# Gathering the adjacency rows that hold something, instead of multiplying all 26 blocks

## The chip, the cores and the metric

The kernel runs on one core of one Trainium2 chip. The metric is the device time of one execution in microseconds (us), lower is better. A profile is one execution with the hardware profiler on; its span is up to 12 us off the median of the timed runs, so sums over stages use spans and verdicts use timed runs.

Engines in the profile: PE is TensorE (PEld its weight loads), DVE is VectorE, ACT is ScalarE, POOL is GpSimd, SP is SyncE. A "q" behind a name is that engine's sequencer, which also issues its DMAs.

## The reference, cut to what matters

`x` is 3327 nodes by 256 features, `adj` is 3327 by 3327 and sparse, all float32. The kernel pads 3327 to 26 blocks of 128.

```python
h = relu(layernorm(x))
R = (adj + I) / rowsum
Xf = Xa = h
for n in range(2):                       # "step 1" and "step 2" below
    A  = top_p_attention(Xa)             # softmax over 3327 nodes, smallest set with 90% of the mass
    Xf = R @ Xf                          # needs adj @ Xf
    Xa = A @ Xa
    Z += Xf @ U1[n].T + Xa @ U2[n].T
x = x + layernorm(h + Z) * g + b
h = relu(layernorm(x))
x = x + relu((d * adj * d.T) @ h @ W.T + bias)     # "stage 3"; d = rowsum ** -0.5
```

So adj is multiplied three times, over the same sparse pattern: 3 x 26 row blocks, each against all 26 column blocks. A row block's 128 rows of adj (transposed: 128 partitions, one per column node of a block) are empty in most (partition, block) places: with these inputs a partition has 7.65 places with something, of 26, on average, and at most 15.

## The kernel before

Per row block, adj arrives in four chunks and is multiplied in full:

```python
def adj_matmul(i, rhs, width):
    acc = ps_r.tile([P, 512], F32, tag="psr", name="adj_acc")
    for b0, nb in ADJ_CHUNKS:                          # 7 + 7 + 7 + 5 blocks
        a = big.tile([P, ADJ_BLOCKS, P], F32, tag="adj", name="adj_sb", bufs=3)
        nc.sync.dma_start(a[...], adj_t[i * P : (i + 1) * P, ...])
        for b in range(nb):
            nc.tensor.matmul(acc[:, :width], a[:, b, :], rhs[b0 + b][:, :width], ...)
    return acc

def tail1(i, e, den, xt):                              # after the attention of block i in step 1
    attend(e, den, h, xa1[i])                          # transpose e, multiply: "attend" below
    key_block(kt2, i, xa1[i])
    acc = adj_matmul(i, h, D + 1)                      # the last column gives the row sums
    t1 = acc[:, D] + 1.0; r_inv[i] = 1 / t1            # the "degree operation", VectorE
    propagate(acc, i, h, xf1[i])
# ... step 2 the same with xf1; stage 3: adj_matmul(i, h, D), scale, project, add, store
```

The attention itself is a chain on VectorE and ScalarE. In `prepare(i+1)` ScalarE exponentiates the logits and makes a start value; VectorE negates it (`nt`, "the negated threshold"), and ScalarE runs two counting passes (`ja`) over 3327 columns. VectorE then narrows the threshold with full-width passes (`scalar_tensor_tensor`, `max8`, `match_replace`). Which instruction stands where on each in-order engine is settled when the program is built, by the recording layer's own estimate of when things are ready.

## Time and profile before

| | us |
|---|---|
| median of 4 runs | 2593.8 (2592.5 to 2595.8) |
| span of the profile | 2595.4 |
| up to the first of the second full-width passes of step 1 | 118.0 |
| step 1, per row block | 36.5 |
| turn, last block of step 1 to first of step 2 | 76.8 |
| step 2, per row block | 42.9 |
| the rest, with stage 3 | 417.1 |

The stage times are starts of the second full-width pass over the scores (one per block and step), so "start", 25 periods of step 1, the turn, 25 periods of step 2 and the rest sum to the span.

### The profile page before, as it was taken

To read this page: it belongs to the slowest core of one execution; us is meant where nothing else is said; L and a number is where in the kernel's file an instruction comes from. 1 tells how busy PE (TensorE), PEld (TensorE's weight loads), DVE (VectorE), ACT (ScalarE), POOL (GpSimd) and SP (SyncE) were. 2 spreads that over 40 slices of the span, in tenths; PEclk is the share of its full clock that TensorE was granted. 3 is DMA by queue.
4 is the path that set the end of the run, shared out by engine and by line. 5 is a ranking of instruction groups with operands and counts; after the bars stand their busy time and mean duration, and the time that the engine had idled before them with its cause. 6 is when DMAs were issued, how large, how long until landed. Compare 5 with 4: busy or idle time off the path is not lost.

```text
span 2595.4 us, 29857 instructions
## 1 busy us (share of the span) xinstructions
PE 2303.9 (89%) x10458; PEld 1782.2 (69%) x10458; DVE 1704.9 (66%) x5071; ACT 971.9 (37%) x2315; POOL 61.2 (2%) x110
## 2 busy tenths in 40 slices
PE   5899999999999999969898989898989885899998
PEld 3677667776777677747676767676767664677776
DVE  3487787778777777488878887888788878000000
ACT  2534544554454444424434443444344433000000
POOL 1000000000000000000000000000000000000000
PEclk8899999999999999989999999999999997999999
DMA  3211111111111111211111111111111100244453
GB/s 106 80 39 46 48 53 39 46 49 52 39 46 53 48 39 53 69 29 43 49 39 54 43 49 39 53 43 49 40 53 43 49 24 9 82 144 140 141 143 102
DMA packets 66386, 153.77 MB, mean 59 GB/s; under 512 B 8116, under 2 KB 26290, under 8 KB 66226
## 3 DMA queue, kind: packets, MB, share of 16 engines
q1 hardware_dynamic: 63600, 149.97, 20.3%
q10 hardware_dynamic: 2626, 1.80, 0.2%
q8 instruction: 84, 1.38, 0.2%
q14 instruction: 76, 0.62, 0.1%
HBM read 144.93 MB, written 6.81 MB: 58 GB/s over the span
## 4 chain that ended last, share of the span: by engine, by line
DVE 53%; PE 30%; ACT 12%; issue 2%; POOL 1%; DMA 1%; ACTq 0%; POOLq 0%; SPq 0%
PE adj_acc L181 17%; DVE cand L335 8%; ACT ja L273 8%; DVE w L301 7%; DVE w L332 7%; DVE w L360 7%; PE att_acc L444 6%; DVE e L362 6%; PE p_t L436 3%; DVE cand L344 3%; DVE val L342 3%; ACT at L439 2%; POOL bn_rr L151 1%; PE p_xt_k L158 1%; PE p_o L541 1%
## 5 line engine op out<-in xcount | busy, mean ns | idle before, releaser
L181 PE MATMUL adj_acc<-h,adj_sb 128*128 128x257 f32 (+1 forms) x2704 | 674.4, 393 | 20.0 <-DVE h L529 10.1
L181 PEld LDWEIGHTS adj_acc<-h,adj_sb 128*128 128x128 f32 x2704 | 500.4, 195 | 98.6 <-issue 18.4
L181 PE MATMUL adj_acc<-xf,adj_sb 128*128 128x256 f32 x1352 | 371.8, 408 | 55.2 <-DVE prop L456 55.2
L439 ACT COPY at<-p_t 128x512 f32<-128x512 f32 (+1 forms) x364 | 184.4, 539 | 488.8 <-PE p_t L436 486.9
L444 PE MATMUL att_acc<-xa,at 128*128 128x256 f32 (+1 forms) x1352 | 334.3, 400 | 5.7 <-ACT at L439 5.7
L436 PE MATMUL p_t<-ident,e 128*128 128x128 f32 x1352 | 205.3, 296 | 136.7 <-DVE e L362 136.7
L444 PE MATMUL att_acc<-h,at 128*128 128x256 f32 (+1 forms) x1352 | 324.4, 391 | 0.6
L181 PEld LDWEIGHTS adj_acc<-xf,adj_sb 128*128 128x128 f32 x1352 | 257.1, 204 | 97.0 <-DVE prop L456 60.2
L273 ACT ACTIVATE ja<-e,nt 128x3327 bf16<-128x3327 f32 x104 | 319.2, 3070 | 5.0 <-DVE nt L269 3.8
L301 DVE SCALAR_TENSOR_TENSOR w<-e,t 128x3327 f32<-128x3327 f32 x78 | 287.3, 3683 | 46.9 <-ACT t L296 46.9
L444 PEld LDWEIGHTS att_acc<-xa,at 128*128 128x128 f32 (+1 forms) x1352 | 264.0, 200 | 65.6 <-ACT at L439 28.4
L444 PEld LDWEIGHTS att_acc<-h,at 128*128 128x128 f32 (+1 forms) x1352 | 258.6, 196 | 58.3 <-ACT at L439 22.9
L436 PEld LDWEIGHTS p_t<-ident,e 128*128 128x128 f32 x1352 | 177.0, 154 | 169.1 <-DVE e L362 151.9
L230 PE MATMUL p_l<-kt,q 64*128 64x512 f32 (+2 forms) x832 | 248.6, 555 | 7.2 <-ACT e L251 1.4
L335 DVE MAX8 cand<-w 128x8 f32<-128x208 f32 x832 | 251.3, 360 | 0.8
L546 DVE SCALAR_TENSOR_TENSOR o<-p_o,x_in 128x256 f32<-128x256 f32 x26 | 11.0, 424 | 345.6 <-PE p_o L542 345.6
L251 ACT ACTIVATE e<-p_l 128x512 f32<-128x512 f32 (+2 forms) x416 | 209.3, 514 | 72.9 <-PE p_l L230 70.2
L230 PEld LDWEIGHTS p_l<-kt,q 64*128 64x128 f32 x832 | 111.6, 185 | 150.3 <-ACT e L251 107.4
L332 DVE SCALAR_TENSOR_TENSOR w<-e,t 128x3327 f32<-128x3327 f32 x52 | 191.6, 3684 | 17.0 <-ACT t L296 16.9
L362 DVE SCALAR_TENSOR_TENSOR e<-w,kept,e 128x3327 f32<-128x3327 f32 x52 | 191.5, 3682 | 0.5
L360 DVE MATCH_REPLACE8 w<-kept,e 128x3335 f32<-128x3335 f32 x52 | 188.1, 3617 | 0.0
L284 DVE TENSOR_SCALAR n<-sign 128x1 f32<-128x1 f32 x52 | 7.9, 151 | 257.2 <-ACT ja L273 257.2
(350 smaller groups left out, 1795.2 us busy)
## 6 DMA issues: line engine op xcount, KB each, us to landing
adj_sb<-in_adj_t SPq DMA_DIRECT2D x234, 448.0 KB, 3.4
adj_sb<-in_adj_t SPq DMA_DIRECT2D x78, 320.0 KB, 2.9
x_in<-in_x SPq DMA_DIRECT2D x50, 128.0 KB, 2.0
x_hbm<-x_in SPq DMA_DIRECT2D x26, 128.0 KB, 2.0
x_in<-x_hbm SPq DMA_DIRECT2D x26, 128.0 KB, 2.1
out<-o SPq DMA_DIRECT2D x25, 128.0 KB, 1.7
u<-in_u1t ACTq DMA_DIRECT2D x2, 256.0 KB, 3.9
u<-in_u2t ACTq DMA_DIRECT2D x2, 256.0 KB, 5.0
```

The lines of the kernel that those rows point to most:

```text
L181: nc.tensor.matmul(acc[:, :width], a[:, b, :], rhs[b0 + b][:, :width], start=(b0 + b == 0), stop=(b0 + b == NB - 1),)
L230: nc.tensor.matmul(pl[:, :w], q[s * DA : (s + 1) * DA, :], kt[s * DA : (s + 1) * DA, c0 : c0 + w], start=True, stop=True,)
L251: nc.scalar.activation(e[:, at : at + w], pl[:, :w], AF.Exp, accum_out=zp[:, n : n + 1])
L273: nc.scalar.activation(ja, e[:, :N], f, bias=nt, accum_out=acc)
L301: nc.vector.scalar_tensor_tensor(jd, ev, t, ev, op0=ALU.is_gt, op1=ALU.mult, accum_out=mass)
L332: nc.vector.scalar_tensor_tensor(w[:, :N], ev, t, ev, op0=ALU.is_le, op1=ALU.mult, accum_out=below)
L335: nc.vector.max(cand[:, 8 * n : 8 * n + 8], w[:, c0 : c0 + cw])
L360: nc.vector.match_replace(w, kept, e, BIG)
L362: nc.vector.scalar_tensor_tensor(ev, w[:, :N], kept[:, 0:1], ev, op0=ALU.is_gt, op1=ALU.mult, accum_out=den)
L436: nc.tensor.transpose(pt[:kb, (b - g0) * P : (b - g0 + 1) * P], a[:, b * P : b * P + kb], ident)
L439: nc.scalar.copy(at[:, :full], pt[:, :full])
L444: nc.tensor.matmul(acc[:, :D], at[:kb, (b - g0) * P : (b - g0 + 1) * P], v[b][:kb, :D], start=(b == 0), stop=(b == NB - 1),)
```

## The change

Its intent: most of the 26 matmuls of a product multiply zeros. So for each row block, list on chip which (partition, block) places hold something, gather just those rows of adj and the matching rows of the operand by indirect DMA, and multiply 10 slots instead of 26 blocks. The list is made once, in step 1; the gathered adj rows go to memory and are reloaded in step 2 and stage 3. Nine slots are a partition's own, the tenth slot is shared: places beyond nine are spread over free partitions of it through a running count (`p_before`) and a permutation by matmul (`p_shared`).

```diff
+    def list_nodes(i):                                  # VectorE: 4 reduces over the dense row
+        for b0, nb, a in adj_chunks(i):                 # adj_sb now has bufs=2
+            nc.vector.tensor_reduce(most[:, b0 : b0 + nb], a[:, :nb, :], AX.X, ALU.max, apply_absolute_value=True)
+        ...                                             # 2 x (max, match_replace) over 26 codes
+        nc.tensor.matmul(before[:, 0:1], tri, count)    # p_before
+    def share_slots(i, codes, there, count, before):
+        nc.vector.tensor_scalar(at, slot_no[:, :OVER], before[:, 0:1], None, op0=ALU.add)   # at_slot
+        nc.vector.tensor_tensor(sel, slot_no..., at..., op=ALU.is_equal)                    # 128 x 896
+        nc.gpsimd.tensor_scalar(rows[:, :, 0], codes, -1.0, terms[:, 0:1], ...)
+        nc.gpsimd.tensor_scalar(rows[:, :, 1], codes, -float(P), terms[:, 1:2], ...)
+        for k in range(OVER):                                                               # p_shared
+            nc.tensor.matmul(shared[:, :2], sel[:, k, :], rows[:, REG + k, :], ...)
+        nc.scalar.copy(rows[:, REG, :], shared[:, :2])
+    def gather_adj(i, rows):
+        nc.gpsimd.tensor_scalar(a_idx, rows...); nc.gpsimd.tensor_scalar(v_idx[:, i, :], rows...)
+        for k in range(SLOTS):                                                              # 10
+            nc.gpsimd.indirect_dma_start(ac[:, k, :], None, adj_t..., a_idx[:, k : k + 1])
+        nc.sync.dma_start(ac_hbm[i * P : (i + 1) * P], ac...)
+    def gather_nodes(i, hbm, width):                                                        # 10
+        for k in range(SLOTS):
+            nc.gpsimd.indirect_dma_start(vg[k][:, :width], None, hbm[:, :], v_idx[:, i, k : k + 1])
+    def adj_gathered(ac, vg, width):
+        for k in range(SLOTS):
+            nc.tensor.matmul(acc[:, :width], ac[:, k, :], vg[k][:, :width], ...)
...
+        def ahead1(i):                                  # in the middle of block i
+            gather1(i + 1); lists[i + 2] = list_nodes(i + 2)
         def tail1(i, e, den, xt):
             attend(e, den, h, xa1[i])
             key_block(kt2, i, xa1[i])
-            acc = adj_matmul(i, h, D + 1)
+            rows[i + 2] = share_slots(i + 2, *lists.pop(i + 2))
+            acc = adj_gathered(*parts.pop(i), D + 1)
...
+        # stage 3: odd blocks gathered, even blocks dense as before
```

Further parts: the reciprocal roots move from GpSimd (`pow`) to ScalarE (Ln, Exp), `h` and step 1's result xf go through memory, and the counting passes write uint8 in place of bf16. The lists hold 16 places a partition and 128 shared ones a block; the kernel checks this at its end, and repeats the whole network dense where it fails. With these inputs they fit (at most 15 places and 75 shared ones).

## The prediction

> **What bounds the kernel now.** I first cut the run into its stages and read the busy time of each engine in each (start:end in us, length, then busy us and instruction counts per engine, granted TensorE clock, DMA share, GB/s):
>
> ```profile
> core 0: us, PE busy (x) PEld busy (x) DVE busy (x) ACT busy (x) POOL busy (x), PEclk, DMA share, GB/s
> 118.00:1030.00 912.00, 849.31 (x3960) 650.57 (x3959) 697.01 (x2041) 428.57 (x997) 16.53 (x24) 0.97 0.17 48
> 1030.00:1107.00 77.00, 74.40 (x349) 57.39 (x348) 38.48 (x115) 31.47 (x77) 0.00 (x0) 1.00 0.25 72
> 1107.00:2215.00 1108.00, 949.46 (x4283) 733.77 (x4282) 910.20 (x2686) 441.99 (x1050) 27.44 (x50) 0.92 0.14 41
> 2215.00:2595.00 380.00, 345.77 (x1545) 281.08 (x1543) 15.48 (x40) 24.38 (x58) 1.09 (x2) 0.98 0.45 128
> ```
>
> The first row is attention step 0 ("step 1" below), then the turn to step 2, step 2 itself, and the last layer ("stage 3"), which multiplies by adj and little else. Each has 26 row blocks. The starts of the second full-width pass over the scores lie 36.2 to 37.2 us apart in step 1 (I use 36.6), some 40.4 and 45.7 us in turn in step 2 (mean 42.9), and stage 3 repeats every 14.0 us.
>
> TensorE is 93% busy in step 1, and that invites the belief that it is the bound. So next I asked what VectorE waits for, over the whole run (us in total, times, longest):
>
> ```profile
> DVE o L546 <- PE p_o L542: 345.6, 26, 14.0
> DVE n L284 <- ACT ja L273: 257.2, 38, 7.1
> ...
> DVE prop L456 <- PE adj_acc L181: 3.8, 2, 3.4
> DVE t L490 <- PE adj_acc L181: 1.8, 1, 1.8
> ```
>
> The first line is stage 3. In steps 1 and 2 the large wait is for ScalarE's two counting passes; the waits for the adj product come to 5.6 us in 52 blocks. So those products are filler: they run in TensorE's gaps and seldom hold VectorE. The order of VectorE's work in one block shows its chain (start, duration, instruction, idle before it and its releaser):
>
> ```profile
> 640.12 3.62 DVE L360 MATCH_REPLACE8 w<-kept,e 128x3335 f32<-128x3335 f32 x1
> 643.77 3.68 DVE L362 SCALAR_TENSOR_TENSOR e<-w,kept,e 128x3327 f32<-128x3327 f32 x1
> ...
> 656.77 0.15 DVE L284 TENSOR_SCALAR n<-sign 128x1 f32<-128x1 f32 x1 [6.48 <-ACT ja L273]
> ```
>
> It is full except for this 6.5 us hole. TensorE in stage 3 is the opposite case:
>
> ```profile
> 2404.04 10.63 PE L181 MATMUL adj_acc<-h,adj_sb 128*128 128x256 f32 x48
> 2415.32 0.44 PE L158 MATMUL p_xt_k<-ident,prop 128*128 128x128 f32 x2 [0.65 <-ACT prop L537]
> 2415.59 1.03 PE L181 MATMUL adj_acc<-h,adj_sb 128*128 128x256 f32 x4
> 2416.46 1.03 PE L541 MATMUL p_o<-w_l,xt_k 128*128 128x256 f32 x4
> 2417.42 0.69 PE L542 MATMUL p_o<-b_l,ones_row 1*128 1x256 f32 x2
> ```
>
> One float32 matmul is two passes, so a product is 52 of them: 11.1 us (52 x 0.2137, the mean from dividing a long run of such matmuls) plus 2.2 us of projection and some 0.7 us of gaps, which is the 14.0. Only here is the adj product the bound.
>
> **What the Trainium skill says.** "Perfetto Trace Analysis", section Identifying the Most-Contended Engine, says that matmul busy share does not tell how near TensorE is to its limit. The trace agrees: 93% busy in step 1, and yet hardly waited for. "DMA: Bandwidth & Descriptors", section SWDGE vs HWDGE vs iDMA, says that GpSimd's DMAs have their descriptors computed in software by a GpSimd core, with a single queue; its section Latency and other measured facts puts the first byte at about 1 us, against 0.6 us on the hardware path, and names the emission of descriptors as the reason. The trace of before cannot confirm either: it has no GpSimd DMA at all (its queues are "hardware_dynamic" and instruction fetches). Its SyncE loads of 448 KB land after 3.4 us, its 128 KB transfers after 1.7 to 2.1 us.
>
> **The change, part by part.**
>
> *Removed.* 16 of 26 matmuls per product: 16 x 2 x 0.2137 = 6.84 us of TensorE per product, in all 52 blocks of steps 1 and 2 and in the 13 odd blocks of stage 3. (26 + 26 + 13) x 6.84 = 445 us of TensorE time, but by the above only stage 3's share is on the path.
>
> *Stage 3.* Even blocks stay at 14.0 us, and may lose some 0.5 us because adj now has two buffers for three: a chunk of 7 takes 7 x 0.4275 = 3.0 us to use and 3.4 us to land. Odd blocks become 14.0 - 6.84 = 7.2. A pair takes 21.7 in place of 28. 13 pairs are 282; with a few us at either end 285 to 295 in place of 380: **-85 to -95**, if the 10 gathers of a pair fit in its 21.7 us.
>
> *VectorE in step 1.* New per block: four reduces over the dense adj row; from a 1664-element reduce of the run before at 1.874 us I take 896 x 1.13 ns = 1.0 us plus a little, so three at 1.08 and one of 640 at 0.82: 4.06. Lists (two rounds of max and replace over 26 codes, some ten small operations) about 1.6, the 128x896 comparison 1.08, a few smalls 0.4: about 7.1 us. In the order of the built program 5.4 of it (reduces and lists) stands between the negated threshold and the counts, that is, in the 6.5 us hole. VectorE's own chain stays near 37 to 38.
>
> *The gather loop of step 1.* This decides. Per block GpSimd makes two index operations and issues 20 indirect DMAs of 128 rows (10 of adj, 10 of the operand) in order. In the built program's order TensorE has, in this sequence: the gathered product A(i), then attend(i-1), the projection for the keys, then the small `p_shared` matmuls that finish the list for block i+1; ScalarE copies these into `rows`; GpSimd's indices for i+1 wait for that copy; A(i+1) waits for the last gather. Engines go in order, so this is a closed ring, once per block:
> - 20 gathers: 20T, with T the GpSimd time of one;
> - landing of the last: about 2.3 us (a 128 KB transfer lands in 1.7 to 2.1 above); its matmul 0.6;
> - attend: 20.6 (from 647.52, the first transposition, to 668.2, the end of its last matmul in before);
> - projection to the end of the keys: 2.7 (to about 670.6, with the adj filler between);
> - 7 small matmuls 1.2, copy 0.6, two GpSimd operations 1.2 (one of 128x1 took 0.55 in before).
>
> Sum: 20T + 29.2. VectorE does not escape: its degree operation behind A(i) also stands right after the last pass over the scores of block i-1, so it stops until A(i) is there. T is in no trace of mine. My estimate is 1.1 us, from the skill's 1 us of emission above, and from the diff gathering only every other block in stage 3: gathering all would make a block the larger of 7.2 and 10T, against 21.7 / 2 = 10.9 with half of them, so the author's choice makes sense only for a T of about 1.1 or more. With T = 1.1 the ring is 51.2, against 36.6: 25.5 periods x 14.6 = **+372**. T = 0.6 gives 41, 0.8 gives 45, 1.5 gives 59.
>
> *Step 2.* The gathers need only the list kept from step 1 and rows in memory, so they run a block ahead: 10T = 11 us of GpSimd in 42.9. VectorE's order is nearly as before: about 0. The reciprocal root moves from GpSimd (0.55 us a call) to two ScalarE operations: 0 to 10 over the run, taken as 0.
>
> *Ends.* The turn took 77 us against a period of 43 with TensorE full; less adj work there gives about -10. At the start of step 1 the first two lists and 20 gathers stand before block 0: about +20.
>
> Sum: 2594 + 372 - 90 - 10 + 20 = 2886; I say **2890 us**.
>
> **The rivals.**
> (a) *Cheap gathers*: with T at most 0.4 the ring is 37 us and hides under VectorE; only stage 3 moves: about 2500. For it: descriptor work may be pipelined within the queue. Against it: the skill's figure, and that stage 3 is half dense.
> (b) *GpSimd's throughput alone*: if my reading of the ring is wrong and the gathers run ahead freely, the period is max(37, 20T + 1.2). At T = 1.1 nothing changes in step 1 and the total is about 2510; at T = 2 it is 41 and the total near 2620. Against it: the built order itself.
> (c) *TensorE is the bound, as its busy share suggests*: then all 445 us come off: about 2150. The wait table speaks against it.
> (d) *The two adj buffers*: reduces wait for loads of 3.4 us per chunk, queued on SyncE behind stores that wait for gathers. The hole absorbs some; worth +2 to +5 per block, 50 to 130 in all, on top of (a) or (b), and mostly hidden inside the ring.
>
> **Range and chances.** T from 0.7 to 1.5 gives rings of 43 to 59, totals of about 2685 to 3095; with (d) a little more above: 2690 to 3130. Faster by over 2% (below 2541) needs T under about 0.5 or no ring: 6%. Within 2% needs T near 0.5 or a mix of (a) with (d): 7%. Slower: 87%.
>
> **What would show it.** The starts of the second full-width pass in step 1 about 51 us apart. VectorE's degree operation waiting for the gathered product, over 10 us a block, the largest new wait of the run; TensorE's gathered product waiting for gather DMAs; GpSimd issuing for 22 us of each period and idle for the rest, its index operations waiting for ScalarE's copy of `rows`. Stage 3 in pairs of about 22 us, step 2 unchanged near 43. It is wrong if GpSimd's 20 gathers take under 9 us or over 30, if they start before the attend of the block before has ended, or if the degree operation does not wait. If GpSimd never idles in step 1, (b) holds and the ring is not the reason.

## The result, and the profile after

| | before | after |
|---|---|---|
| median, us | 2593.8 | 3121.9 (4 runs, 3116.3 to 3135.3) |
| ratio | | 1.204 (95%: 1.200 to 1.208) |

A ratio is the mean time of one kernel's fast runs over that of the other's in the same rounds, so it is not quite the ratio of the medians quoted. The change is slower by a fifth. That lies inside the predicted range, near its upper end (3130).

The stages of the profile after, in the same columns as the table in the prediction (step 1, turn, step 2, rest):

```profile
198.00:1572.00 1374.00, 955.43 (x3528) 645.15 (x3528) 816.65 (x2384) 440.60 (x1068) 555.13 (x574) 0.74 0.25 73
1572.00:1681.00 109.00, 77.25 (x251) 49.98 (x249) 37.86 (x107) 32.44 (x77) 44.98 (x46) 0.70 0.24 73
1681.00:2717.00 1036.00, 807.74 (x3526) 599.93 (x3526) 884.16 (x2580) 454.90 (x1140) 345.82 (x214) 0.93 0.18 56
2717.00:3114.00 397.00, 301.17 (x1223) 229.68 (x1221) 38.59 (x105) 30.54 (x76) 123.24 (x130) 0.90 0.43 131
```

In step 1 no engine is full any more: TensorE 70%, VectorE 59%, ScalarE 32%, GpSimd 40%. When nothing is full and the time is longer, the engines wait for one another, perhaps in a circle. Who waits for whom, over the run and all engines (us in total, times, longest):

```profile
POOL a_idx L288 <- ACT rows L281: 757.6, 25, 88.2
...
DVE t L641 <- PE adj_acc L317: 320.4, 23, 17.9
DVE o L729 <- PE p_o L725: 244.2, 18, 20.7
PE adj_acc L317 <- DMA vg<-h_hbm,v_idx: 240.9, 121, 9.7
...
DVE n L417 <- ACT ja L406: 63.0, 11, 7.1
```

The old large wait (the counting passes, 257.2) has shrunk to 63.0, and the degree operation `t`, which waited 1.8 us in all before, now waits 320.4, some 14 us each time. It waits for the gathered product, that waits for gathers, and GpSimd's index operation waits for `rows`, once per block. One turn of the circle, from GpSimd's timeline and then TensorE's:

```profile
746.78 1.03 POOL L292 DMA_INDIRECT ac<-in_adj_t,a_idx  x1 [0.27 <-POOL v_idx L289]
748.12 0.95 POOL L292 DMA_INDIRECT ac<-in_adj_t,a_idx  x1 [0.30 <-issue]
...
773.94 0.95 POOL L308 DMA_INDIRECT vg<-h_hbm,v_idx  x1 [0.30 <-issue]
...
802.33 0.26 POOL L288 TENSOR_SCALAR a_idx<-rows 128x10 int32<-128x10 f32 x1 [26.82 <-ACT rows L281]
```

```profile
776.01 2.23 PE L317 MATMUL adj_acc<-vg,ac 128*128 128x257 f32 x4 [0.33 <-DMA vg<-h_hbm,v_idx]
778.03 1.50 PE L569 MATMUL p_t<-ident,e 128*128 128x128 f32 x8
...
799.15 0.71 PE L328 MATMUL p_k<-xt_k,w 128*128 128x128 f32 x4 [0.46 <-ACT xt_k L199]
800.30 1.70 PE L280 MATMUL p_shared<-rows,sel 128*128 128x2 f32 x14 [0.44 <-ACT kt L333]
```

Twenty gathers from 746.8 to 774.9, the last two slots' matmuls to 778.2, attend and the key projection to 799.9, the shared-slot matmuls to 802.0, and GpSimd, idle for 26.82 us, starts the next indices at 802.33: 56.4 us after the last time (745.93). The turn is a typical one: the mean over 21 turns of step 1 is 56.1 us, with 27.9 for the gathers.

Where the time went, by the five stage numbers of the two profiles:

| stage | before | after | difference |
|---|---|---|---|
| start | 118.0 | 198.0 | +80.0 |
| step 1, 25 periods | 911.7 (36.5 each) | 1374.3 (55.0 each) | +462.6 |
| turn | 76.8 | 108.9 | +32.1 |
| step 2, 25 periods | 1071.8 (42.9) | 1035.3 (41.4) | -36.5 |
| rest | 417.1 | 397.9 | -19.2 |
| span | 2595.4 | 3114.5 | +519.0 |

### The profile page after: what moved, and what is told of

It is laid out like the page before. It is cut to its first block, busy times and chain, and to the rows that moved or that the text cites. A ratio compares the mean times of both kernels' runs of the same rounds, so it can differ in the third digit from the quotient of the medians.

```text
span 3114.5 us, 28889 instructions
## 1 busy us (share of the span) xinstructions
PE 2231.8 (72%) x8794; PEld 1582.5 (51%) x8794; DVE 1857.8 (60%) x5442; ACT 1019.7 (33%) x2549; POOL 1113.0 (36%) x1026
## 4 chain that ended last, share of the span: by engine, by line
issue 31%; PE 28%; DVE 17%; POOL 10%; ACT 7%; DMA 5%; another core or an unknown queue 1%; SPq 0%; POOLq 0%; ACTq 0%
PE att_acc L577 11%; POOL ac L292 5%; PE adj_acc L225 4%; POOL vg L308 4%; PE adj_acc L317 4%; DVE w L493 3%; DVE e L495 2%; DMA vg<-h_hbm,v_idx 2%; ACT ja L406 2%; PE p_t L569 2%; DMA adj_sb<-in_adj_t 2%; DVE w L434 2%; PE p_l L363 1%; ACT at L572 1%; DVE cand L468 1%
## 5 line engine op out<-in xcount | busy, mean ns | idle before, releaser
L317 PE MATMUL adj_acc<-vg,ac 128*128 128x256 f32 (+1 forms) x1300 | 467.2, 498 | 303.5 <-DMA vg<-h_hbm,v_idx 240.9
L308 POOL DMA_INDIRECT vg<-xf_hbm,v_idx x260 | 393.7, 1514 | 635.3 <-PE adj_acc L317 559.1
L317 PEld LDWEIGHTS adj_acc<-vg,ac 128*128 128x128 f32 x1300 | 278.2, 237 | 464.4 <-issue 231.4
L577 PE MATMUL att_acc<-xa,at 128*128 128x256 f32 (+1 forms) x1352 | 355.6, 418 | 49.1 <-ACT at L572 48.0
L406 ACT ACTIVATE ja<-e,nt 128x3327 uint8<-128x3327 f32 x104 | 319.3, 3070 | 57.1 <-DVE nt L402 42.3
L363 PE MATMUL p_l<-kt,q 64*128 64x512 f32 (+2 forms) x832 | 303.7, 698 | 34.1 <-ACT q L357 22.8
L308 POOL DMA_INDIRECT vg<-h_hbm,v_idx x260 | 281.1, 1081 | 87.9 <-issue 71.6
L292 POOL DMA_INDIRECT ac<-in_adj_t,a_idx x260 | 284.0, 1092 | 78.3 <-issue 67.8
L434 DVE SCALAR_TENSOR_TENSOR w<-e,t 128x3327 f32<-128x3327 f32 x78 | 287.3, 3684 | 19.6 <-ACT t L429 16.0
L308 POOL DMA_INDIRECT vg<-hn_hbm,v_idx x130 | 123.2, 948 | 375.2 <-DMA hn_hbm<-h 186.3
L225 PE MATMUL adj_acc<-h,adj_sb 128*128 128x256 f32 x676 | 171.2, 410 | 54.4 <-DMA adj_sb<-in_adj_t 44.7
```

The costliest lines, as they stand in the source:

```text
L225: nc.tensor.matmul(acc[:, :width], a[:, b, :], rhs(b0 + b)[:, :width], start=(b0 + b == 0), stop=(b0 + b == NB - 1),)
L292: nc.gpsimd.indirect_dma_start(ac[:, k, :], None, adj_t.rearrange("r (b n) -> (r b) n", n=P), bass.IndirectOffsetOnAxis(ap=a_idx[:, k : k ...
L308: nc.gpsimd.indirect_dma_start(vg[k][:, :width], None, hbm[:, :], bass.IndirectOffsetOnAxis(ap=v_idx[:, i, k : k + 1], axis=0))
L317: nc.tensor.matmul(acc[:, :width], ac[:, k, :], vg[k][:, :width], start=(k == 0), stop=(k == SLOTS - 1))
L363: nc.tensor.matmul(pl[:, :w], q[s * DA : (s + 1) * DA, :], kt[s * DA : (s + 1) * DA, c0 : c0 + w], start=True, stop=True,)
L406: nc.scalar.activation(ja, e[:, :N], f, bias=nt, accum_out=acc)
```

## The experiments

All experiments were right in their results unless said otherwise. Their stage numbers, to be read with the texts below:

| kernel | median us | start | step 1 each | turn | step 2 each | rest |
|---|---|---|---|---|---|---|
| before | 2593.8 | 118.0 | 36.5 | 76.8 | 42.9 | 417.1 |
| after | 3121.9 | 198.0 | 55.0 | 108.9 | 41.4 | 397.9 |
| e1_order | 2968.3 | 195.8 | 49.1 | 102.1 | 41.4 | 402.0 |
| e2_half (wrong on purpose, one look) | 2861.1 | 170.2 | 45.7 | 107.0 | 41.5 | 402.3 |
| e3_bufs (one look) | 3058.2 | 196.2 | 55.4 | 96.8 | 41.5 | 342.4 |
| e4_dense1 | 2936.2 | 131.5 | 50.8 | 98.8 | 41.5 | 404.4 |
| e5_behind | 2703.1 | 155.2 | 42.9 | 86.4 | 41.5 | 355.6 |
| e6_ring1 (one look) | 3109.5 | 156.6 | 58.9 | 88.5 | 41.4 | 355.4 |
| v1 | 2576.7 | 124.9 | 38.9 | 111.7 | 42.0 | 316.4 |
| v2 | 2494.3 | 120.6 | 36.5 | 97.5 | 41.6 | 313.3 |
| e7_spare (one look) | 2598.4 | 118.2 | 36.6 | 93.0 | 42.2 | 413.7 |

### e1_order: the gathered product moved behind the attend

```diff
+    with tc.issue_after(last_shared[i + 1]):     # queue on TensorE behind p_shared of block i+1
         acc = adj_gathered(*parts.pop(i), D + 1)
```

> Only the place of the gathered product of block i on TensorE changes: in step 1 (blocks 1 to 24) it is queued behind the shared-slot matmuls of block i+1, so after the attend of block i-1. Ring theory: nothing in the list for block i+1 waits for block i's gathers any more, GpSimd's 28 us per block run beside everything else, and the period of step 1 falls from 55.0 us to 37 to 40; the run to about 2690 to 2780 us. Rival 1 (GpSimd's own throughput sets the period) and rival 2 (VectorE's new list work sets it): the period stays at 50 or more, the run within 2% of 3122.

Measured: 2968.3 us, ratio to before 1.144; step 1 at 49.1 us on average and 51 in its steady part. A miss for both sides: the ring was cut where the theory said, the run gained 154 us, and step 1 was still 13 us a block above the kernel before. Two waits of VectorE's timeline in this run show what took its place:

```profile
820.19 0.23 DVE L268 TENSOR_SCALAR at_slot<-slot_no,p_before 128x7 f32<-128x7 f32 x1 [7.24 <-PE adj_acc L320]
...
835.79 0.19 DVE L253 MAX8 codes<-most 128x8 f32<-128x26 f32 x1 [5.71 <-issue]
```

The first is a 0.23 us operation of the list for a later block. It stands in VectorE's queue just before the `match_replace` that ends the present block, and it waits for `p_before`, a matmul on one column, which stands on TensorE behind the logits. (The built program lets it wait for nothing else; `adj_acc` is only what the profile shows at its release.) Not all of its wait is queue order: in most blocks of this run it is released 2 to 10 us after the end that the profile models for `p_before` (820.2 against 817.7 here), with little or no work shown on TensorE in the longer of these stretches. Why TensorE was late there is left open. The second begins as GpSimd's two small list operations end (835.76), which stand in GpSimd's queue behind the 20 gathers (in the built order this instruction has a semaphore wait on GpSimd, so the "issue" of the profile, meaning that it saw no releaser, is this wait). So the trace suggests a second circle, through the bookkeeping of the list: attend, logits and `p_before` on TensorE, `at_slot` before the end of the block on VectorE, the next attend.

### e2_half: half the gathers in step 1

```diff
-        for k in range(SLOTS):            # in gather_adj, and likewise in gather_nodes for step 1
+        for k in range(0, SLOTS, 2):
```

> Wrong results on purpose: step 1 gathers 5 + 5 rows per block in place of 10 + 10 and multiplies 5; order and list work as in the changed kernel. Ring theory: each gather stands on the ring with its 1.25 us, so the period falls by 10 x 1.25 plus some 1.5 us of the occasional slow gather, from 55 to 41 to 42, and the run to about 2770 us. If the gathers were beside the path: no change. If VectorE's list work is the bound: no change.

Measured: 2861.1 us, step 1 at 45.7 us a block, alternating between 43 and 49. The gathers are on the path, as they should be, but ten of them gave back 9.3 us where the ring alone promised 13 to 14. The trace shows what kept the rest. Over 21 turns the gathers take 13.9 us on average in place of 27.9, but the attend begins 7.9 us after the last gather in place of 3.2, because now TensorE waits for `e`, the pass with which VectorE ends a block (waits from 400 to 1300 us):

```profile
PE p_t L573 <- DVE e L499: 89.9, 10, 13.1
```

In the changed kernel this wait does not occur between 400 and 1300 us. So a second path, through VectorE, holds the period about 5 us above what the ring alone would give here; e5 and e6 then take the two apart.

### e3_bufs: three buffers for adj

```diff
-    a = big.tile(..., tag="adj", name="adj_sb", bufs=2)     ... tag="vg", bufs=14
+    a = big.tile(..., tag="adj", name="adj_sb", bufs=3)     ... tag="vg", bufs=10
```

> Three buffers for adj as in the kernel before, ten for gathered operand rows in place of fourteen. If the two adj buffers cost stage 3 its gain: a pair of blocks takes 21.7 to 22.5 us in place of 25.5, and the run falls by 40 to 50 us; the ring of step 1 stays at 55. Rival: the loads stand in SyncE's queue behind the store of the previous output, whatever their number: pairs stay at 25 to 26, the run the same.

Measured: 3058.2 us; a pair of blocks of stage 3 takes 21.4 us in place of 25.5, and step 1 does not move (55.4). The run fell by 64 us, more than the 40 to 50 expected: the rest by 55.5, of which 11 are in the first pair of blocks, and the turn by 12. An even, dense block of stage 3 on TensorE, first in the changed kernel and then here:

```profile
2850.67 5.45 PE L225 MATMUL adj_acc<-h,adj_sb 128*128 128x256 f32 x24
2859.82 7.13 PE L225 MATMUL adj_acc<-h,adj_sb 128*128 128x256 f32 x24 [3.71 <-DMA adj_sb<-in_adj_t]
```

```profile
2853.97 10.92 PE L225 MATMUL adj_acc<-h,adj_sb 128*128 128x256 f32 x48
```

With two buffers TensorE stops for 3.71 us in the middle of the block, and the second half then takes 7.13 us for the 5.45 of the first: after a pause the same matmuls are slower. The Trainium skill, "TensorE: Matmul & The Clock Gate", Part 1, says that the clock follows how busy TensorE has been, and the traces agree: the granted clock over the slower half is 0.76, over the first half 1.00; and in e5_behind, where the pause is 1.29 us, the 24 passes after it take 5.45. So a stall can cost more than its length. In step 1 the granted clock fell from 0.97 before to 0.74 after; the prediction had left this out. With three buffers there is one run of 48. The prediction had allowed 0.5 us for this. A later run shows that the number of buffers is only a part of this: e5_behind has two buffers too, and stops for only 1.3 to 1.5 us (22.6 us a pair), because there the load of the third chunk was issued when the first chunk was through, at 2497.1 for a block begun at 2492.2; in the changed kernel it was issued only when the second was, at 2856.2 for a block begun at 2848.2. So the count of buffers costs about 1 us a pair, and which of the two the third chunk was given costs the other 3. That the recording layer gave it the wrong one is read from these issue times, not tested by itself.

### e4_dense1: step 1 multiplies all 26 blocks again

```diff
-    acc = adj_gathered(*parts.pop(i), D + 1)
+    acc, lists = list_nodes(i, lambda b: h[b], D + 1)   # dense product and reduces over the same chunks
+    gather_adj(i, share_slots(i, *lists))               # 10 gathers, for step 2 and stage 3 only
```

> Step 1 multiplies all 26 blocks again, and still makes the lists and gathers the adj rows (10 indirect DMAs a block) for step 2 and the last layer; steps 2 and 3 as in the changed kernel. 6.84 us more TensorE work per block and no product waits for a gather. Ring theory: step 1's period is VectorE's chain, 37 to 39; no 80 us at the start; the run about 2540 to 2620. Rival 2 (VectorE's list work sets the period): 7 us on top of 36.6, so 43 to 45, the run 2700 or more. TensorE as the bound: slower than the changed kernel, over 3122.

Measured: 2936.2 us, ratio 1.130; step 1 at 50.8. The start fell to 131.5, as expected, but with no product waiting for any gather, step 1 was as slow as in e1. VectorE and SyncE in one period:

```profile
774.65 1.09 DVE L253 TENSOR_REDUCE most<-adj_sb 128x7 f32<-128x896 f32 x1 [7.60 <-DMA adj_sb<-in_adj_t]
```

```profile
755.98 0.33 SPq L644 DMA_DIRECT2D xf_hbm<-xf  x1
769.68 0.33 SPq L302 DMA_DIRECT2D ac_hbm<-ac  x1
770.17 1.36 SPq L214 DMA_DIRECT2D adj_sb<-in_adj_t  x2
```

SyncE issues nothing for 13 us: the store of the gathered rows stands at the head of its queue and waits for the gathers to land, and the loads of adj stand behind it; 0.5 us after the store they go. VectorE's reduce waits 7.60 us for such a load, with the negated threshold behind it. So the gathers reached VectorE through a third in-order queue. That is the first half of step 1. From the block at 871 us on, the reduces hardly wait for chunks, and the next list waits in their place, 4.9 to 11.5 us a block:

```profile
1079.21 0.19 DVE L259 MAX8 codes<-most 128x8 f32<-128x26 f32 x1 [11.52 <-issue]
```

It begins as GpSimd's two list operations end (1079.18), which stand behind the block's gathers, as in e1_order, and the period stays at 49 to 54 us up to the last two blocks. So one queue held step 1 in the first half and the other in the second. My first theory, that the ring closes through the product alone, fell here.

### e5_behind and e6_ring1: the bookkeeping out of the way, with and without the product's ring

e5_behind is e1_order with the list's work placed where VectorE idles, the two list operations taken from GpSimd, and the store on GpSimd's queue. e6_ring1 is the same with only e1's edit undone.

```diff
+    with tc.issue_after(last_nt[0]):                 # VectorE: behind the negated threshold
         lists[i + 2] = list_nodes(i + 2)
+    with tc.issue_after(last_e[0]):                  # VectorE: behind the pass that ends the block
         at_slot, crowd, sel
-    nc.gpsimd.tensor_scalar(rows[...]) x2
+    nc.vector.tensor_scalar(rows[...]) x2
-    nc.sync.dma_start(ac_hbm[...], ac)
+    nc.gpsimd.dma_start(ac_hbm[...], ac)
```

> e1_order left step 1 at 51 us. Theory now: a second ring, through VectorE's and GpSimd's queues. VectorE's slot operation stands before the pass that ends block i (match-replace and e) and waits for the small count matmul, which stands on TensorE behind the logits; and GpSimd's two list operations stand behind 20 gathers, with VectorE's next list waiting for them. This kernel is e1_order with the list work placed where VectorE has its hole (behind the negated threshold), the two list operations on VectorE, and the store of the gathered rows on GpSimd's queue. If the second ring is all: step 1 at 38 to 41 us, the run at 2700 to 2770. Rival: GpSimd's descriptor writing and VectorE's passes hold each other up, whatever the order: 47 or more, the run over 2880.

> e5_behind, with only the gathered product put back to its old place (before the attend of the block before). The ring of the prediction alone: 28 us of gathers, 3 of landing and last matmul, 20 to 22 of attend, 4 to 6 of projection, shared-slot matmuls and indices: 54 to 57 us a block, the run 3080 to 3160, as slow as the changed kernel although nothing of the second ring is left. If the prediction's ring were not binding by itself: under 50, the run under 3000.

Measured: e5_behind 2703.1 us, ratio 1.042; step 1 at 42.9 (the run inside what was expected, the period 2 us over it). e6_ring1 3109.5 us, step 1 at 58.9, 2 us over the 54 to 57 expected: the attend takes 22.4 us on average there, 19.0 in the changed kernel. With the changed kernel and e1 this makes a square for the period of step 1:

| | product before the attend | product behind it |
|---|---|---|
| list work as built | 55.0 (after) | 49.1 (e1) |
| list work moved | 58.9 (e6) | 42.9 (e5) |

Either circle alone holds the period at 49 or more (in e1_order some of it may be TensorE's unexplained lateness); only without both does it fall. That is why cutting the one that the prediction named gave so little by itself, and it also refutes the rival that GpSimd's descriptor writing and VectorE's passes hold each other up to 47 us or more whatever the order. The second row changes three things at once (places on VectorE, GpSimd's list operations, the queue of the store), so what each of them is worth is not shown. What keeps e5 6 us above the kernel before is in its waits: over the run VectorE waits 90.8 us for adj chunks and 76.2 for exponentials.

### v1 and v2: a version that beats both

If gathers in step 1 only cost, step 1 can stay dense, and the list be made there with no hurry: it is wanted only in step 2. v1 does this (lists one to two blocks behind, behind the negated threshold), with e5's store, three adj buffers, and two of every three blocks of stage 3 gathered. v2 adds two repairs that v1's profile asked for.

```diff
 v1, step 1 (from e4_dense1):
+    if i > 1: gather_adj(i - 2, share_slots(i - 2, *lists.pop(i - 2)))
+    if i:     lists[i - 1] = code_nodes(i - 1, mosts.pop(i - 1))     # all behind last_nt on VectorE
+    acc, mosts[i] = list_nodes(i, lambda b: h[b], D + 1)
 v1, stage 3:
-    if sparse and i % 2:
+    if sparse and i % 3:                  # gathered rows in the idle score tiles
 v2:
-    adj_sb bufs=3, vg bufs=10
+    adj_sb bufs=5, vg in the same buffers, three rows to a tile
-    lists and gathers of blocks 24 and 25 in the turn
+    in blocks 1 and 2 of step 2
```

> Made to beat both: step 1 dense as in e4_dense1, lists one to two blocks behind and in VectorE's hole, store of gathered rows on GpSimd's queue, three adj buffers, and in the last layer two of every three blocks gathered (20 gathers = 25 to 27 us of GpSimd in 14.0 + 7.2 + 7.2 = 28.4 us). Ring theory: step 1 at 37.5 to 40 us; step 2 at 41.4 as in the changed kernel; three blocks of the last layer in 28.5 to 30 us; the run 2480 to 2560, against 2594 of the kernel before. Rival: TensorE, which was 93% busy in step 1, has no room for the 3 us of list matmuls: step 1 at 41 or more and the run no better than 2594.

Measured: 2576.7 us, ratio 0.993 (0.990 to 0.995): better than before by 0.7%, the same by a 2% measure, and short of the 2480 to 2560 expected. Step 1 (38.9) and stage 3 (28.1 us for three blocks) were as expected, step 2 nearly (42.0 for 41.4); the miss is the turn, 111.7 us, where three blocks' lists and gathers stood one after the other.

> v1 with two things mended that its trace shows. The turn to step 2 took 111.7 us against 76.8 before, because the lists and gathers of the last three blocks stood in it one after the other: the last two are now made in step 2. And VectorE's reduces waited 1.4 us a block for adj chunks: adj has five buffers in place of three, shared with the gathered operand rows of step 2. Expected: the turn at 80 to 92 us, step 1 at 38 to 39.5 us in place of 39.3, the rest as in v1; the run 2520 to 2560, against 2577 of v1 and 2594 of the kernel before. Rival: TensorE (95% busy in v1's step 1) is the bound there now, and buffers change nothing: step 1 stays at 39.3 and only the turn is gained, 2550 to 2560.

Measured over 5 runs: 2494.3 us (2484.1 to 2499.3), ratio 0.962 (0.961 to 0.964), faster than before by 3.8% and than expected, because step 1 came down to 36.5 us, to the tenth what it was in the kernel before. VectorE between the threshold and the count:

```profile
725.45 0.15 DVE L422 TENSOR_SCALAR nt<-t 128x1 f32<-128x1 f32 x1 [0.24 <-ACT t L420]
...
726.04 1.07 DVE L289 TENSOR_TENSOR sel<-slot_no,at_slot 128x896 f32<-128x896 f32 x1
...
728.13 3.79 DVE L253 TENSOR_REDUCE most<-adj_sb 128x7 f32<-128x896 f32 x4
732.08 0.15 DVE L437 TENSOR_SCALAR n<-sign 128x1 f32<-128x1 f32 x1 [0.16 <-ACT ja L426]
```

The 6.5 us hole of the kernel before is filled with 6.4 us of list work, and the count still waits 0.16 us for ScalarE: the whole list costs nothing. TensorE is 96% busy over five such blocks (176.42 of 183.70 us) with the list's matmuls added to the dense product, and the period is the old one, so the rival (TensorE as the bound) fell. More buffers also changed the built order, and the run does not tell these two apart. The turn (97.5) is above the 80 to 92 expected, and still 21 us above before.

### e7_spare: why step 2 became faster

```diff
+        for n in range(16):                # before the product of step 2, sum thrown away
+            nc.tensor.matmul(acc[:, :width], ac[:, n % SLOTS, :], vg[n % SLOTS][:, :width], ...)
```

> Step 2 fell from 42.9 to 41.4 us a block in the changed kernel and in every experiment, which the prediction had put at 0. This is v2 with 16 further matmuls in front of each product of step 2, whose sum is thrown away (results stay right), so that TensorE does the 26 of the kernel before. If TensorE's lighter load is the reason: step 2 back at 42.5 to 43.2 us a block, the run 30 to 45 us above v2's 2494. Rival (the root moved from GpSimd to ScalarE, or the operand now coming through memory, is the reason): step 2 stays at 41.4, the run within 10 us of v2.

Measured: step 2 at 42.2 us on average. Over 16 steady periods (the eighth to the 23rd) it is 42.1, against 41.7 in v2 and 43.3 before. So, in one look, TensorE's lighter load accounts for about a quarter of the gain (0.4 of 1.6 us), and neither side of the expectation holds. The run as a whole is no measure: it lost 100 us in stage 3, which was not touched, where single matmuls stand 1.4 us apart with TensorE waiting for nothing that the profile shows. That is left open.

## Why the prediction was right or wrong

**What bounds the kernel before: right.** The prediction took the adj product for filler in steps 1 and 2. v2 shows it twice: step 1 has the same 36.5 us with the dense product and list matmuls added, and the change, with 6.84 us less TensorE work per block, was slower.

**The gather loop: right in its mechanism, short in one term, and not alone.** The ring is there as drawn, in the waits and the timeline (56.4 us for one turn), and e6_ring1 has it without the second circle at 58.9. Its terms, predicted and measured in the turn shown above:

| term | predicted | measured |
|---|---|---|
| 20 gathers | 22 (T = 1.1) | 28.1 |
| landing and last matmul | 2.9 | 3.1 |
| attend | 20.6 | 19.7 |
| to the end of the keys | 2.7 | 2.2 |
| shared-slot matmuls, copy, indices | 3.0 | 3.3 |
| sum | 51.2 | 56.4 |

The term that was mis-sized is T. A gather keeps GpSimd for 0.95 us, not far from the 1 us of emission that the estimate started from, but the next one starts 0.30 us later, so it is 1.25 each, and one of the twenty as a rule takes 3 to 4 us (last section). Step 1 therefore took 462.6 us more over its 25 periods; the prediction put 372. That 1.1 came so near is partly luck: the skill's figure is the time to a first byte, not the time between two gathers, and the other ground was a guess at why the author gathers every other block.

What the prediction did not see is the second circle. It had read from the built order that the list's work on VectorE falls into the hole, and took the chain as 37 to 38 us without the ring. The order had this right for the reduces, but one small slot operation stood before the end of the block and waited for TensorE, and GpSimd's list operations stood behind the gathers. For the total it did not matter, since the first circle was the longer one; for whoever would have mended the kernel by the prediction, it did: e1_order stopped at 49.

**Start: the size was off.** +20 was predicted, +80 measured. The prediction charged two lists and 20 gathers. In the trace there are 40: GpSimd runs the gathers of two blocks, from 122 to 183 us, before block 0 reaches its second pass at 198. e4_dense1, v1 and v2, whose first blocks wait for no gathers, start at 131.5, 124.9 and 120.6.

**Turn: the sign was wrong.** -10 was predicted for less TensorE work, +32 measured. In the trace VectorE's additions for the first gathered products of step 2 stand before its last pass of step 1, and wait 7.4 and 16.7 us (for the second the profile names no releaser), while the gathers of these products cannot start before the last result of step 1 is in memory. This cause is read from the trace; no run tests it alone.

**Step 2: the size was off.** 0 was predicted, -36.5 measured. e7_spare gives a quarter of it to TensorE's lighter load; the rest is open.

**Stage 3: the gain was right and was then lost to the buffers.** Pairs of 21.7 us were predicted, 25.5 measured, and 21.4 with a third buffer in e3_bufs. The step that failed is "may lose some 0.5 us", where 4 us a pair were lost. That cost 11 x 4.1 = 45 us over the steady pairs. The gathers did fit: 10 take 12.5 us of a pair. With three buffers the rest is 342.4, against 327 by the prediction (417 less 90); these 15 us are not explained.

**The rivals.** (a), cheap gathers, and (c), TensorE as the bound, are excluded: T is 1.25, and less TensorE work did not help. (b), GpSimd's throughput, is excluded by GpSimd's 26.82 us of idling per block. (d), adj buffers and SyncE's queue behind stores that wait for gathers, was called mostly hidden inside the ring. That is how it is: it surfaced as soon as the ring was gone, in e4_dense1. But it was put at 2 to 5 us a block, and there the reduce alone waits some 7.4 to 8.6 us a block for the load, until GpSimd's list operations take its place.

So the range held, but because it was wide and not because errors cancelled: four of the five were too low, and only step 2 went the other way. They are: step 1 (+91 against the prediction), start (+60), turn (+42), stage 3 (+71, counting all of the rest), step 2 (-37): 227 in all, which is the 519 measured less the 292 predicted.

## What to carry to other kernels

Less work on an engine pays only where that engine is waited for; find that in the waits, not in the busy share. When data-dependent gathers are put into a software pipeline, write down the closed circle of in-order queues that they run through, the small operations above all: a 0.2 us operation in front of a large one can carry a circle of its own, and a store that waits for a gather can hold up every load behind it. And put new work into a hole whose end is set by another engine, where it costs nothing, rather than remove work that nobody waits for.

## What the Trainium skill lacked or had wrong

- "DMA: Bandwidth & Descriptors", section Latency and other measured facts, has a first byte of about 1 us for a DMA issued by GpSimd; no page that I read says how many indirect DMAs GpSimd can issue. Here one of 128 rows keeps it for 0.95 us, and the next follows 0.30 us later: one every 1.25 us, whether the rows have 512 or 1024 bytes.
- "SBUF — State Buffer", section Who interferes with whom, says that a VectorE instruction with two SBUF inputs contends with a GpSimd instruction that reads SBUF. It does not count the issue of an indirect DMA among those; here it behaves like one, and I had not charged it. Of the 910 gathers of the changed kernel 79 took over 1.8 us: 77 began during a full-width `scalar_tensor_tensor` pass (3.68 us, two inputs) and ended about 0.82 us after it, and two during the two-input comparison (`sel`), in which ten others began and were not slow. Three more began during such a pass and were not slow: one in its last us (1.76 us), and two within 0.05 us of its start, for which I have no reason. The gathers that began inside `match_replace` (100) or a run of `max8` (31) took at most 1.03 us. In this pair, from the timeline of all engines, the gather starts 0.16 us into the pass:

```profile
813.11 3.67 DVE L495 SCALAR_TENSOR_TENSOR e<-w,kept,e 128x3327 f32<-128x3327 f32 x1
813.27 4.32 POOL L292 DMA_INDIRECT ac<-in_adj_t,a_idx  x1 [0.31 <-issue]
```
